# Two selective-scan instructions of 448 tokens joined into one of 898 columns, with the carried state in a column between them

## The chip, the cores and the metric

The kernel runs on one core of one Trainium2 chip. The metric is the device time of one execution in microseconds, from its first to its last instruction. The kernel before takes 8633.8 us, the median of three runs from 8621.33 to 8647.61. Engine names below: PE is the matrix engine, DVE the vector engine, ACT the scalar engine, POOL is GpSimd, and SP starts the transfers.

## The reference, cut to what matters

Four layers work on four images of 56 x 56 tokens and 96 channels. The last two are attention and a small feed-forward part. The first two hold a selective scan, and that scan fills nearly all of the time. Per image it runs in four directions (rows or columns, forward or backward), for 192 channels with 16 states each, over 3136 tokens:

```python
dt  = softplus(dts + dt_bias)
dA  = exp(dt * A)                 # one decay for each token, channel and state
dBu = dt * B * u                  # what a token adds
def step(h, inp):
    dA_l, dBu_l, C_l = inp
    h = dA_l * h + dBu_l          # the recurrence, token after token
    return h, einsum('bkdn,bkn->bkd', h, C_l)
_, ys = lax.scan(step, h0, (dA, dBu, Ct))
```

Everything around it (projections, convolutions, norms, the feed-forward parts) is matrix work and elementwise work, which the kernel runs in the gaps.

## The kernel before

The kernel cuts each direction into 7 steps of 448 tokens. A step has 8 rounds (two halves of the channels, four sets of states), which makes 2 layers x 4 images x 4 directions x 7 steps x 8 rounds = 1792 rounds. In a round 3 groups of 128 (channel, state) pairs are scanned, each in one DVE instruction over the tokens. One round consists of

- two or three products on DVE, `v = du * b` (L673). In 1204 rounds the third one is done ahead of time on POOL (L651);
- three scans on DVE, in place in `v`, with decays read from PSUM (L699);
- three exponentials on ACT, which write the next round's decays into PSUM as soon as the scan that read the old ones is through (L643);
- two small copies on ACT: the state that ends a step goes out to `carry` (L703), and the state that begins the next round's step comes in from `carry` (L658);
- the product with C on POOL over all three groups (L709), and on PE the sum over states.

```python
CS = 448
TOKENS = slice(1, CS + 1)
...
        da = [self.psum.tile([128, 512], F32, name=f"da{g}")[:, : CS + 2] for g in range(NG)]
        for t in da:
            nc.vector.memset(t, 0.0)

        def decay(n, g):
            ch, e, q = rounds[n]
            nc.scalar.activation(da[g][:, TOKENS], ch.dt[e][:, g], AF.Exp, scale=ch.par.na[:, e, q, g : g + 1])

        def begin(n):
            ch, e, q = rounds[n]
            b = self.spread_b(ch, q)
            v = sp.tile([128, NG, CS + 2], F32, name="v", bufs=3)
            ahead = NQ * e + q not in (OWN_TAIL if ch.l and ch.i else OWN)
            if ahead:
                nc.gpsimd.tensor_tensor(v[:, 2, TOKENS], ch.du[e][:, 2], ch.cb[q][:, 1], ALU.mult)
            return b, v, ahead

        def carried(n, v):
            ch, e, q = rounds[n]
            at = CS + 1 if ch.rev else 0
            if ch.step:
                nc.scalar.copy(v[:, :, at : at + 1], ch.par.carry[:, e, q].unsqueeze(2))
        ...
        for n, (ch, e, q) in enumerate(rounds):
            ...
            c = 1 if ch.step else 0
            way = slice(CS + c, 0, -1) if ch.rev else slice(1 - c, CS + 1)
            end = 1 if ch.rev else CS
            b, v, ahead = nxt
            for g in range(2 if ahead else 3):
                nc.vector.tensor_tensor(v[:, g, TOKENS], ch.du[e][:, g], b, ALU.mult)
            ...
            yield "F", n, r                    # other lanes may put ACT work here
            ...
            if more:
                nxt = begin(n + 1)
            ...
            for g in range(NG):
                if g == 1:
                    yield "C", n, r            # other lanes may put PE and DVE work here
                ...
                nc.vector.tensor_tensor_scan(
                    v[:, g, way], da[g][:, way], v[:, g, way], 0.0, ALU.mult, ALU.add
                )
                if g == 2 and ch.step < NCS - 1:
                    nc.scalar.copy(ch.par.carry[:, e, q].unsqueeze(2), v[:, :, end : end + 1])
                if more:
                    decay(n + 1, g)
                    if g == 0:
                        carried(n + 1, nxt[1])
            hc = sp.tile([128, NG, CS], F32, name="hc", bufs=3)
            nc.gpsimd.tensor_tensor(hc, v[:, :, TOKENS], ch.cb[q][:, 0].unsqueeze(1).to_broadcast([128, NG, CS]), ALU.mult)
```

The order of instructions on each engine is the order in which this code emits them. The waits between engines are set by the framework, from the overlap of the stretches of a tile that two instructions touch. "Lanes" are the other layers' parts (projections, norms, feed-forward), which are let in at the two `yield`s. A scan writes `h` over `v`. Where a step continues a direction, the column ahead of the first token holds the carried state, and since its decay is zero the scan starts from it.

Of the kernel before, what the change touches and what calls it, by code (L numbers as in the profile page):

```python
# [11 lines left out]
F32 = mybir.dt.float32  # L12
# [3 lines left out]
AF = mybir.ActivationFunctionType  # L16
ALU = mybir.AluOpType
# [9 lines left out]
NG = 3  # L27
NQ = 4
# [2 lines left out]
CR = CW // HS  # L31
NCW = L // CW
CS = 448
TOKENS = slice(1, CS + 1)
NCS = L // CS
RANK = (12, 6)
NW, LATE_NW = 13, 20
# [6 lines left out]
BANKS, LATE_BANKS = 2, 4  # L44
# [120 lines left out]
class Net:  # L165
# [25 lines left out]
    def late(self):  # L191

        self.scan_pool.close()
        self.wp = self.pool("late", bufs=2)
        self.nw, self.nwin, self.depth, self.banks = LATE_NW, LATE_DEPTH, LATE_DEPTH, LATE_BANKS
        tags = (("ps", BANKS), ("da0", 1), ("da1", 1), ("da2", 1), ("pp", 1), ("b", 1), ("y", 1))
        self.ring = cycle([t for t in tags for _ in range(t[1])])

    def ps(self):
# [395 lines left out]
    def scans(self):  # L595

        nc, sp = self.nc, self.sp
        chunks = []
        for l in range(2):
            for i in range(NB):
                for n, (orient, rev) in enumerate(ORDER[l]):
                    for step in range(NCS):
                        ch = Step()
                        ch.l, ch.i, ch.orient, ch.rev, ch.step = l, i, orient, rev, step  # L610
                        ch.k = 2 * orient + rev if l == 0 else orient + 2 * rev
                        ch.c = NCS - 1 - step if rev else step
                        ch.n, ch.first = n, n == 0 and step == 0
                        ch.skip = n == 0
                        ch.last = n == 3 and step == NCS - 1
                        for n_ in ("dt", "du", "cb", "dtc", "duc", "dtd", "dud"):
                            setattr(ch, n_, [])
                        chunks.append(ch)
        first, second = chunks[:2]
        self.parameters(first)  # L620
        self.inputs(first)
        self.project_step(first, 0)
        self.project_step(first, 1)
        for r in range(8):
            if r:
                self.prepare(Step(), first, r)
            self.prepare_on_scalar(first, r)
        self.parameters(second)
        self.project_step(second, 0)
        self.project_step(second, 1)  # L630
        rounds = [(ch, e, q) for ch in chunks for e in range(NE) for q in range(NQ)]
        nexts = dict(zip(chunks, chunks[1:]))
        afters = dict(zip(chunks, chunks[2:]))


        da = [self.psum.tile([128, 512], F32, name=f"da{g}")[:, : CS + 2] for g in range(NG)]
        for t in da:
            nc.vector.memset(t, 0.0)

        def decay(n, g):  # L640

            ch, e, q = rounds[n]
            nc.scalar.activation(da[g][:, TOKENS], ch.dt[e][:, g], AF.Exp, scale=ch.par.na[:, e, q, g : g + 1])  # L643

        def begin(n):
            ch, e, q = rounds[n]
            b = self.spread_b(ch, q)
            v = sp.tile([128, NG, CS + 2], F32, name="v", bufs=3)
            ahead = NQ * e + q not in (OWN_TAIL if ch.l and ch.i else OWN)
            if ahead:  # L650
                nc.gpsimd.tensor_tensor(v[:, 2, TOKENS], ch.du[e][:, 2], ch.cb[q][:, 1], ALU.mult)  # L651
            return b, v, ahead

        def carried(n, v):
            ch, e, q = rounds[n]
            at = CS + 1 if ch.rev else 0
            if ch.step:
                nc.scalar.copy(v[:, :, at : at + 1], ch.par.carry[:, e, q].unsqueeze(2))  # L658

        nxt = begin(0)  # L660
        self.exp_and_ln()
        self.tables = True
        for g in range(NG):
            decay(0, g)
        late = []
        for n, (ch, e, q) in enumerate(rounds):
            r = NQ * e + q
            c = 1 if ch.step else 0
            way = slice(CS + c, 0, -1) if ch.rev else slice(1 - c, CS + 1)
            end = 1 if ch.rev else CS  # L670
            b, v, ahead = nxt
            for g in range(2 if ahead else 3):
                nc.vector.tensor_tensor(v[:, g, TOKENS], ch.du[e][:, g], b, ALU.mult)  # L673
            self.prepare(ch, nexts.get(ch), r)
            self.half_round()
            far = afters.get(ch)
            strided = [1.5 + 1.5 * ch.orient] * (r % NQ == 2)
            if far and self.projected(far, r) in (0, 1):
                strided.append(1.5 + 1.5 * far.orient)
            self.spend((0.7, 0, 1.3, 1.3, 0, 0, 0, 0)[r], 1.3 * (r in (1, 3)) + sum(strided))  # L680
            yield "F", n, r
            self.prepare_on_scalar(nexts.get(ch), r)
            ended = late.pop(0) if len(late) == 2 else None
            if ended:
                self.keep_busy(ended[2])
            more = n + 1 < len(rounds)
            if more:
                nxt = begin(n + 1)
            if ended:
                self.add_up(*ended)  # L690
            self.prepare_ahead(afters.get(ch), r)
            self.half_round()
            for g in range(NG):
                if g == 1:
                    yield "C", n, r
                if g == 2 and ended and ended[2] == NQ - 1:
                    self.spend(0.6, 0)
                    self.keep_sums(*ended[:3])
                nc.vector.tensor_tensor_scan(  # L699
                    v[:, g, way], da[g][:, way], v[:, g, way], 0.0, ALU.mult, ALU.add  # L700
                )
                if g == 2 and ch.step < NCS - 1:
                    nc.scalar.copy(ch.par.carry[:, e, q].unsqueeze(2), v[:, :, end : end + 1])  # L703
                if more:
                    decay(n + 1, g)
                    if g == 0:
                        carried(n + 1, nxt[1])
            hc = sp.tile([128, NG, CS], F32, name="hc", bufs=3)
            nc.gpsimd.tensor_tensor(hc, v[:, :, TOKENS], ch.cb[q][:, 0].unsqueeze(1).to_broadcast([128, NG, CS]), ALU.mult)  # L709
            late.append((ch, e, q, hc))  # L710
        for ended in late:
            self.add_up(*ended)
        self.keep_sums(ch, e, q)
        yield "C", len(rounds), 0
# [624 lines left out]
```

## Time and profile before

| engine | busy us of 8626.1 | in the stage of the rounds, 120 to 8290 us |
|---|---|---|
| DVE | 7939.4 | 7846.7 of 8170 |
| POOL | 7594.3 | 7556.1 of 8170 |
| PE | 7475.5 | 7111.6 of 8170 |
| ACT | 5909.3 | 5686.5 of 8170 |

The first 120 us prepare the first image. The last 336 us are the end of the last lanes, after the last scan. Between them lie the 1792 rounds, 8164 us from the first round's scan to the last one's, or 4.56 us each. In a line of the profile's groups, the first number after the bar is the busy time in us, the next one the mean of one instruction in ns, and after the second bar stands the engine's idle time just before these instructions and who ended most of it.

### The profile page before, as it was taken

Reading aid. Unit: us, or ns where it says so; the run is one execution under the profiler, and the core shown is the slowest. Engines: PE = TensorE matmul, PEld = TensorE weight load, DVE = VectorE, ACT = ScalarE, POOL = GpSimd, SP = SyncE. Lnnn points to the kernel's source line nnn. Section 1 sums busy time; section 2 is a strip of 40 time slices with the busy share of each in tenths; the row PEclk is TensorE's granted clock in tenths of the full one; section 3 lists DMA queues with packets and bytes.
Section 4 is the critical chain, followed back from the end, with each engine's and each line's share of the span. In section 5 each row is a group of like instructions: output and inputs, shape, how many; then the busy total and the mean of one; then the engine's idle time right before and its main releaser. Section 6 shows DMA issues by size and latency. Waiting matters only on the chain. (4 is left out here: it accounts for less than half of the span.)

```text
span 8626.1 us, 120872 instructions
## 1 busy us (share of the span) xinstructions
PE 7475.5 (87%) x33459; PEld 2708.0 (31%) x33459; DVE 7939.4 (92%) x10933; ACT 5909.3 (69%) x12541; POOL 7594.3 (88%) x4075
## 2 busy tenths in 40 slices
PE   6788888898889888898889989988899888998997
PEld 3222223232333223232223223323233232333345
DVE  5999999999999999999999999999999999999951
ACT  5777667676777667776677756667766777667646
POOL 4888989999999999999999999999999999999940
PEclk8888889898999989998899989988899888998987
DMA  5677677677777777776777777667776677766731
GB/s 144 159 184 174 164 179 179 162 167 166 187 169 179 168 185 173 172 176 159 185 175 171 170 174 166 161 154 167 185 174 150 161 165 186 171 149 163 168 90 45
DMA packets 951340, 1417.89 MB, mean 164 GB/s; under 512 B 176578, under 2 KB 943812, under 8 KB 949796
## 3 DMA queue, kind: packets, MB, share of 16 engines
q1 hardware_dynamic: 949888, 1408.37, 68.6%
q8 instruction: 263, 4.31, 0.2%
q14 instruction: 417, 3.42, 0.2%
q10 hardware_dynamic: 772, 1.80, 0.1%
HBM read 1141.42 MB, written 268.14 MB: 163 GB/s over the span
## 5 line engine op out<-in xcount | busy, mean ns | idle before, releaser
L709 POOL TENSOR_TENSOR hc<-v,cb 128x1344 f32<-128x1344 f32 x1792 | 5168.2, 2885 | 499.4 <-DVE v L699 288.1
L699 DVE TENSOR_TENSOR_SCAN v<-da,v 128x449 f32<-128x449 f32 (+1 forms) x5376 | 5523.8, 1072 | 60.4 <-ACT v L658 33.2
L643 ACT ACTIVATE da<-dt,na 128x448 f32<-128x448 f32 x5376 | 3394.5, 633 | 1583.2 <-DVE v L699 1557.3
L673 DVE TENSOR_TENSOR v<-du,b 128x448 f32<-128x448 f32 x4172 | 2330.0, 605 | 136.5 <-PE b L580 50.0
L737 PE MATMUL y<-hc,four 128*32 128x448 f32 x14336 | 1959.6, 622 | 4.3 <-POOL hc L709 4.3
L580 PE MATMUL b<-cf,sel 128*128 128x448 bf16 x1792 | 682.6, 381 | 954.7 <-DVE v L673 949.9
L651 POOL TENSOR_TENSOR v<-du,cb 128x448 f32<-128x448 f32 x1204 | 1374.6, 1142 | 95.8 <-DMA cb<-cd 69.0
L724 PE MATMUL y<-w,zeros 128*96 128x448 bf16 x5117 | 1441.9, 399 | 0.0
L724 PEld LDWEIGHTS <-zeros 128*96 128x96 bf16 x5117 | 631.5, 134 | 1306.5 <-issue 1149.6
L737 PEld LDWEIGHTS y<-hc,four 128*32 128x32 f32 x14336 | 297.5, 114 | 1291.2 <-issue 917.7
L428 PE MATMUL pp<-U,wd 96*128 96x448 f32 x896 | 671.3, 836 | 9.1 <-DMA U<-u 9.1
L733 PE MATMUL y<-Y,ident 96*96 96x448 f32 x672 | 539.8, 892 | 42.3 <-ACT Y L744 23.6
L496 POOL TENSOR_TENSOR duc<-dtc,U 96x448 f32<-96x448 f32 x448 | 559.8, 1250 | 4.6 <-ACT dtc L490 4.6
L886 PE MATMUL ps<-win,dg 64*64 64x220 f32 (+9 forms) x1962 | 509.3, 454 | 0.0
L703 ACT COPY carry<-v 128x3 f32<-128x3 f32 x1536 | 299.2, 195 | 287.7 <-DVE v L699 286.9
L480 PE MATMUL pp<-cf,wd 12*96 12x448 f32 (+1 forms) x896 | 488.0, 627 | 1.1 <-ACT cf L467 1.0
L489 ACT ACTIVATE dtc<-pp,wd 96x448 f32<-96x448 f32 x448 | 279.3, 623 | 270.1 <-PE pp L480 267.7
L593 POOL TENSOR_TENSOR cf<-cf 64x448 f32<-64x448 f32 x448 | 417.5, 932 | 35.7 <-ACT cf L467 0.6
L744 ACT COPY Y<-y 96x448 f32<-96x448 f32 x448 | 339.3, 757 | 31.8 <-PE y L737 30.6
L886 PEld LDWEIGHTS ps<-win,dg 64*64 64x64 f32 (+2 forms) x1962 | 230.6, 158 | 329.9 <-issue 272.7
L580 PEld LDWEIGHTS <-sel 128*128 128x128 bf16 x1792 | 186.7, 104 | 350.2 <-issue 285.8
L733 PEld LDWEIGHTS y<-Y,ident 96*96 96x96 f32 x672 | 116.8, 184 | 553.2 <-ACT da L643 243.8
(426 smaller groups left out, 6066.0 us busy)
## 6 DMA issues: line engine op xcount, KB each, us to landing
cb<-cd SPq DMA_DIRECT2D x3584, 112.0 KB, 4.3
dt<-dd SPq DMA_DIRECT2D x1792, 168.0 KB, 4.4
du<-dd SPq DMA_DIRECT2D x1792, 168.0 KB, 4.2
dd<-dtc SPq DMA_DIRECT2D x448, 168.0 KB, 2.0
dd<-duc SPq DMA_DIRECT2D x448, 168.0 KB, 2.1
U<-u SPq DMA_DIRECT2D x112, 168.0 KB, 4.6
z<-w SPq DMA_DIRECT2D x56, 224.0 KB, 3.1
u<-w SPq DMA_DIRECT2D x56, 224.0 KB, 3.4
```

Of the source, the lines that this page charges most:

```text
L428: self.nc.tensor.matmul(ch.ps.rearrange("p (a b) -> p a b", b=HS), ch.par.wx[:, e], self.in_order(self.U[e], ch.orient, ch.c * CS, CS), st ...
L496: self.nc.gpsimd.tensor_tensor(du.rearrange("p (a b) -> p a b", b=HS), ch.dtc[e].rearrange("p (a b) -> p a b", b=HS), self.in_order(self.U ...
L580: self.nc.tensor.matmul(ps, self.sel[:, q], self.upper(ch.cf), start=True, stop=True)
L643: nc.scalar.activation(da[g][:, TOKENS], ch.dt[e][:, g], AF.Exp, scale=ch.par.na[:, e, q, g : g + 1])
L651: nc.gpsimd.tensor_tensor(v[:, 2, TOKENS], ch.du[e][:, 2], ch.cb[q][:, 1], ALU.mult)
L673: nc.vector.tensor_tensor(v[:, g, TOKENS], ch.du[e][:, g], b, ALU.mult)
L699: nc.vector.tensor_tensor_scan(v[:, g, way], da[g][:, way], v[:, g, way], 0.0, ALU.mult, ALU.add)
L709: nc.gpsimd.tensor_tensor(hc, v[:, :, TOKENS], ch.cb[q][:, 0].unsqueeze(1).to_broadcast([128, NG, CS]), ALU.mult)
L724: self.nc.tensor.matmul(self.y[:C], self.zeros, self.some, start=False, stop=False)
L733: nc.tensor.matmul(o, w, self.in_order(a, ch.orient, ch.c * CS, CS), start=True, stop=False)
L737: nc.tensor.matmul(self.y[32 * n : 32 * n + 32], self.four, hc[:, g], start=n == 3, stop=n == 3 or q == NQ - 1,)
L886: self.nc.tensor.matmul(o[:, a - r0 : e - r0, x0:x1], diag[:, tap], win[:, a + dy - lo : e + dy - lo, x0 + dx : x1 + dx], start=n == 0, st ...
```

## The change

The scans of groups 1 and 2 become one instruction. For that `v` loses its third dimension: it is a row of 3 x 449 + 1 columns, in which one column for the carried state and 448 tokens alternate. The decays of groups 1 and 2 lie in one tile over two adjacent PSUM banks, placed so that each exponential still writes within one bank. Between the two groups of decays stays one column with zero: there the running product is wiped out and the second group's carried state taken up. The column is now needed in every round, so where a direction begins the carried state is a copy of zeros (`none`), which the kernel before did without. The aim is to issue fewer instructions on the vector engine.

```diff
-TOKENS = slice(1, CS + 1)
+GW = CS + 1
...
-        tags = (("ps", BANKS), ("da0", 1), ("da1", 1), ("da2", 1), ("pp", 1), ("b", 1), ("y", 1))
+        tags = (("ps", BANKS), ("da0", 1), ("da", 1), ("pp", 1), ("b", 1), ("y", 1))
...
+        one = self.psum.tile([128, 512], F32, name="da0")[:, : GW + 1]
+        two = self.psum.tile([128, 1024], F32, name="da")[:, 511 - GW : 512 + GW]
+        factors = [one[:, 1:GW], two[:, 1:GW], two[:, 1 + GW : 2 * GW]]
+
+        def tokens(v):
+            return v[:, 1:].rearrange("p (g t) -> p g t", t=GW)[:, :, :CS]
...
-            v = sp.tile([128, NG, CS + 2], F32, name="v", bufs=3)
+            v = sp.tile([128, NG * GW + 1], F32, name="v", bufs=3)
...
         def carried(n, v):
             ch, e, q = rounds[n]
-            at = CS + 1 if ch.rev else 0
-            if ch.step:
-                nc.scalar.copy(v[:, :, at : at + 1], ch.par.carry[:, e, q].unsqueeze(2))
+            at = v[:, 1:] if ch.rev else v[:, : NG * GW]
+            at = at.rearrange("p (g t) -> p g t", t=GW)[:, :, CS if ch.rev else 0]
+            nc.scalar.copy(at.unsqueeze(2), ch.par.carry[:, e, q].unsqueeze(2) if ch.step else none)
...
-            for g in range(NG):
-                if g == 1:
+            for g, f, w in ((0, one, v[:, : GW + 1]), (1, two, v[:, GW:])):
+                if g:
                     yield "C", n, r
...
-                nc.vector.tensor_tensor_scan(
-                    v[:, g, way], da[g][:, way], v[:, g, way], 0.0, ALU.mult, ALU.add
-                )
-                if g == 2 and ch.step < NCS - 1:
-                    nc.scalar.copy(ch.par.carry[:, e, q].unsqueeze(2), v[:, :, end : end + 1])
+                way = slice(f.shape[1] - 1, 0, -1) if ch.rev else slice(0, f.shape[1] - 1)
+                nc.vector.tensor_tensor_scan(w[:, way], f[:, way], w[:, way], 0.0, ALU.mult, ALU.add)
+                if g and ch.step < NCS - 1:
+                    nc.scalar.copy(ch.par.carry[:, e, q].unsqueeze(2), tokens(v)[:, :, end : end + 1])
                 if more:
-                    decay(n + 1, g)
+                    for m in ((0,), (1, 2))[g]:
+                        decay(n + 1, m)
                     if g == 0:
                         carried(n + 1, nxt[1])
```

(The products and the product with C use `tokens(v)` in place of `v[:, :, TOKENS]`; these lines are cut.)

More of the change, by code (lines that the diff above doesn't have):

```diff
@@ L633, in scans @@
         afters = dict(zip(chunks, chunks[2:]))
-        da = [self.psum.tile([128, 512], F32, name=f"da{g}")[:, : CS + 2] for g in range(NG)]
-        for t in da:
-            nc.vector.memset(t, 0.0)
+        none = self.const.tile([128, NG, 1], F32, name="none")
+        nc.vector.memset(none, 0.0)
+        one = self.psum.tile([128, 512], F32, name="da0")[:, : GW + 1]
+        two = self.psum.tile([128, 1024], F32, name="da")[:, 511 - GW : 512 + GW]
+        nc.vector.memset(one, 0.0)
+        nc.vector.memset(two, 0.0)
+        factors = [one[:, 1:GW], two[:, 1:GW], two[:, 1 + GW : 2 * GW]]
+        def tokens(v):
+            return v[:, 1:].rearrange("p (g t) -> p g t", t=GW)[:, :, :CS]
         def decay(n, g):
             ch, e, q = rounds[n]
-            nc.scalar.activation(da[g][:, TOKENS], ch.dt[e][:, g], AF.Exp, scale=ch.par.na[:, e, q, g : g + 1])
+            nc.scalar.activation(factors[g], ch.dt[e][:, g], AF.Exp, scale=ch.par.na[:, e, q, g : g + 1])
         def begin(n):
@@ L647, in begin @@
             b = self.spread_b(ch, q)
-            v = sp.tile([128, NG, CS + 2], F32, name="v", bufs=3)
+            v = sp.tile([128, NG * GW + 1], F32, name="v", bufs=3)
             ahead = NQ * e + q not in (OWN_TAIL if ch.l and ch.i else OWN)
             if ahead:
-                nc.gpsimd.tensor_tensor(v[:, 2, TOKENS], ch.du[e][:, 2], ch.cb[q][:, 1], ALU.mult)
+                nc.gpsimd.tensor_tensor(tokens(v)[:, 2], ch.du[e][:, 2], ch.cb[q][:, 1], ALU.mult)
             return b, v, ahead
@@ L655, in carried @@
             ch, e, q = rounds[n]
-            at = CS + 1 if ch.rev else 0
-            if ch.step:
-                nc.scalar.copy(v[:, :, at : at + 1], ch.par.carry[:, e, q].unsqueeze(2))
+            at = v[:, 1:] if ch.rev else v[:, : NG * GW]
+            at = at.rearrange("p (g t) -> p g t", t=GW)[:, :, CS if ch.rev else 0]
+            nc.scalar.copy(at.unsqueeze(2), ch.par.carry[:, e, q].unsqueeze(2) if ch.step else none)
         nxt = begin(0)
+        carried(0, nxt[1])
         self.exp_and_ln()
@@ L667, in scans @@
             r = NQ * e + q
-            c = 1 if ch.step else 0
-            way = slice(CS + c, 0, -1) if ch.rev else slice(1 - c, CS + 1)
-            end = 1 if ch.rev else CS
+            end = 0 if ch.rev else CS - 1
             b, v, ahead = nxt
             for g in range(2 if ahead else 3):
-                nc.vector.tensor_tensor(v[:, g, TOKENS], ch.du[e][:, g], b, ALU.mult)
+                nc.vector.tensor_tensor(tokens(v)[:, g], ch.du[e][:, g], b, ALU.mult)
             self.prepare(ch, nexts.get(ch), r)
@@ L692, in scans @@
             self.half_round()
-            for g in range(NG):
-                if g == 1:
+            for g, f, w in ((0, one, v[:, : GW + 1]), (1, two, v[:, GW:])):
+                if g:
                     yield "C", n, r
[L696 to L699, printed above, removed]
-                    v[:, g, way], da[g][:, way], v[:, g, way], 0.0, ALU.mult, ALU.add
-                )
-                if g == 2 and ch.step < NCS - 1:
-                    nc.scalar.copy(ch.par.carry[:, e, q].unsqueeze(2), v[:, :, end : end + 1])
+                    if ended and ended[2] == NQ - 1:
+                        self.spend(0.6, 0)
+                        self.keep_sums(*ended[:3])
+                way = slice(f.shape[1] - 1, 0, -1) if ch.rev else slice(0, f.shape[1] - 1)
+                nc.vector.tensor_tensor_scan(w[:, way], f[:, way], w[:, way], 0.0, ALU.mult, ALU.add)
+                if g and ch.step < NCS - 1:
+                    nc.scalar.copy(ch.par.carry[:, e, q].unsqueeze(2), tokens(v)[:, :, end : end + 1])
                 if more:
-                    decay(n + 1, g)
+                    for m in ((0,), (1, 2))[g]:
+                        decay(n + 1, m)
                     if g == 0:
@@ L708, in scans @@
             hc = sp.tile([128, NG, CS], F32, name="hc", bufs=3)
-            nc.gpsimd.tensor_tensor(hc, v[:, :, TOKENS], ch.cb[q][:, 0].unsqueeze(1).to_broadcast([128, NG, CS]), ALU.mult)
+            nc.gpsimd.tensor_tensor(hc, tokens(v), ch.cb[q][:, 0].unsqueeze(1).to_broadcast([128, NG, CS]), ALU.mult)
             late.append((ch, e, q, hc))
```

## The prediction

> **What bounds the kernel now.** I read the busy shares first, then the stage of the rounds by itself, then the groups of instructions, and at last single rounds in the timeline. The page's slices and the stretches (the three rows are the start, the rounds and the end; columns PE, PEld, DVE, ACT, POOL) say where the time lies:
>
> ```profile
> DVE  5999999999999999999999999999999999999951
> POOL 4888989999999999999999999999999999999940
> ...
> 120.00:8290.00 8170.00, 7111.57 (x31932) 2486.02 (x31935) 7846.66 (x10624) 5686.54 (x12068) 7556.10 (x4031) 0.90 0.72 170
> ```
>
> In the rounds DVE is busy for 7846.7 of 8170 us (96%) and idle for 323 us; POOL is at 92.5%, ACT at 70%. So DVE sets the pace, with POOL close behind. The groups:
>
> ```profile
> L709 POOL TENSOR_TENSOR hc<-v,cb 128x1344 f32<-128x1344 f32 x1792 | 5168.2, 2885 | 499.4 <-DVE v L699 288.1
> L699 DVE TENSOR_TENSOR_SCAN v<-da,v 128x449 f32<-128x449 f32 (+1 forms) x5376 | 5523.8, 1072 | 60.4 <-ACT v L658 33.2
> L643 ACT ACTIVATE da<-dt,na 128x448 f32<-128x448 f32 x5376 | 3394.5, 633 | 1583.2 <-DVE v L699 1557.3
> L673 DVE TENSOR_TENSOR v<-du,b 128x448 f32<-128x448 f32 x4172 | 2330.0, 605 | 136.5 <-PE b L580 50.0
> L651 POOL TENSOR_TENSOR v<-du,cb 128x448 f32<-128x448 f32 x1204 | 1374.6, 1142 | 95.8 <-DMA cb<-cd 69.0
> ```
>
> The scan hardly waits (60.4 us over 5376), the exponentials wait for the scans. Now one backward round, first its DVE, then ACT, then POOL:
>
> ```profile
> 2553.17 3.05 DVE L699 TENSOR_TENSOR_SCAN v<-da,v 128x449 f32<-128x449 f32 x3
> 2556.14 1.12 DVE L673 TENSOR_TENSOR v<-du,b 128x448 f32<-128x448 f32 x2
> 2557.19 3.05 DVE L699 TENSOR_TENSOR_SCAN v<-da,v 128x449 f32<-128x449 f32 x3
> ...
> 2554.29 0.64 ACT L643 ACTIVATE da<-dt,na 128x448 f32<-128x448 f32 x1 [1.85 <-DVE v L699]
> 2554.87 0.18 ACT L658 COPY v<-carry 128x3 f32<-128x3 f32 x1
> ...
> 2556.18 1.13 POOL L651 TENSOR_TENSOR v<-du,cb 128x448 f32<-128x448 f32 x1
> ```
>
> Three scans take 2556.14 - 2553.17 = 2.97 us from issue to issue, 0.99 each; the 1.07 us of the group view overlap. Two products take 1.05 us. A round with two products is 4.02 us (2557.19 - 2553.17), and the third product's 0.52 makes it 4.54. The carried state (L658) is in at 2555.05, over a microsecond before the round's products begin, and it is needed only by the scan. And one forward round whose ACT also has lane work:
>
> ```profile
> 1806.70 1.66 DVE L673 TENSOR_TENSOR v<-du,b 128x448 f32<-128x448 f32 x3
> 1808.27 1.08 DVE L699 TENSOR_TENSOR_SCAN v<-da,v 128x449 f32<-128x449 f32 x1
> ...
> 1803.55 1.28 ACT L1033 ACT_TABLE_LOAD   x1
> 1804.85 0.63 ACT L1033 ACTIVATE w<-ps,c 128x448 f32<-128x448 f32 x1
> 1805.50 1.28 ACT L768 ACT_TABLE_LOAD   x1
> 1806.80 0.64 ACT L643 ACTIVATE da<-dt,na 128x448 f32<-128x448 f32 x1
> 1807.37 0.18 ACT L658 COPY v<-carry 128x3 f32<-128x3 f32 x1
> ```
>
> Lane work with two table loads holds ACT from 1803.55 to 1806.78. The first group's exponential and the carried copy come after it, at 1807.55, while DVE has been in its products since 1806.70. Today that is harmless: the scan begins at 1808.27.
>
> [...]
>
> **The change part by part.**
>
> 1. *One scan less per round.* 898 columns are 2 x 449, [...] **-98 us**, all on DVE, the bound. In the steps that begin a direction the scans grow from 448 to 449 columns, 2 ns each, and 256 copies of zeros of 0.18 us are added on ACT: nothing that counts.
>
> 2. *Both exponentials after the joined scan.* Before, the second group's ran beside the third scan; now ACT begins it one scan later and ends both some 0.64 us (one exponential) later. They are needed when the joined scan starts, one scan (0.99 us) earlier than the third group's were. Put on the recorded starts round by round, the joined scan would come too early in 288 rounds, by 119 us in sum. Most of these rounds also have a stall of point 3 ahead of it, so I count half: **+60 us**. The later ACT lane work counts in point 4.
>
> 3. *New waits around the carried copy.* In the built program of the change the copy's target is a strided view of a flat row, and it is ordered against everything between its first and last column. In forward rounds the columns are 0, 449 and 898, so the **first product** of the round now waits for the copy on ACT. In backward rounds they are 449, 898 and 1347, so the **second product** waits for the copy, and the copy waits for POOL's third product where there is one (it writes columns 899 to 1346). None of these waits is in the program before, where the scan alone waited for the copy. Again round by round on the recorded starts, with 0.18 us for the copy[...]:
>  - 895 forward rounds: the copy would be late in 215, by 185 us in sum. In the forward round shown, 1807.55 against 1806.70 makes 0.9 us.
>  - 294 backward rounds without POOL's product: 47 late, 34 us.
>  - 602 backward rounds with it: 335 late, 338 us. In the one shown POOL ends at 2557.31, the copy could end at 2557.54, and the second product began at 2556.65: 0.9 us. POOL's lateness carries over from round to round, and a stall that has pushed DVE back once is not paid again in the next round, so I choose half: 169 us.
>  In sum **+388 us**.
>
> 4. *What shifts behind that.* In the 215 late forward rounds the exponentials of point 2 push lane work, and so the next copy, up to 0.64 us later: at most 138 us, I take half, **+69 us**. In backward rounds ACT stands still for POOL, 1.7 us on average over the 602 rounds, mostly in time in which it waits for scans today. In return, part of the present 323 us of idle DVE is swallowed by the new stalls; I take a third, **-100 us**.
>
> 5. *The end.* The lanes after the last scan rotate over seven PSUM tiles in place of eight. 336 us; I count nothing.
>
> Sum: -98 + 60 + 388 + 69 - 100 = +319, from 8633.8 to 8953. Because two of the halves are chosen and repeated rounds recover more easily than single ones, I round down to **8930 us**.
>
> **Rivals.**
>
> - *The waits are met in time and the saving comes through.* For it: ACT is idle for 30% of the rounds, and the median forward copy would be 1 us early. Then 8634 - 98 = 8536, under 2% in any case. Against it: a quarter of forward and over half of POOL-fed backward rounds are late in the recorded order, and DVE has no slack to hide that.
> - *POOL takes over as the bound.* The loop over two rounds, product with C 2.89, product ahead 1.14, copy 0.18, second product 0.53, first scan 0.99, [...] is 7.95 us, or 3.97 per round; each POOL side job (0.93 or 1.25 us) adds to it, up to 4.6. That is as long as today's 4.56. If it closes in every backward round, the full 338 us count and more: 9100 to 9150.
> - *Only the decays matter*, the new copy waits being covered by them: then about 8634 - 98 + 119 = 8655, within 2%.
> - *Crossing the bank costs something in the scan.* Nothing in the trace tells; 0.1 us per round would be 180 us, on top.
>
> **Range and chances.** With the whole of the absorbed halves gone the sum is about +150 (8790); with all of point 3 and 4 counted it is near +500 (9130). So 8780 to 9120. Slower by over 2% means above 8806: 0.88. Within 2%: 0.10. Faster by over 2%[...]: 0.02.
>
> **What would show it.** In the profile of the changed kernel: [...] DVE's products idle for 300 to 600 us with ACT's carried copy as the releaser (136.5 us in all now, 50.0 of it by PE's b); ACT's copy waiting for POOL's third product by hundreds of us; DVE's share down to some 88 to 89%; rounds near 4.7 us. Were the products' wait for ACT under 100 us, point 3 would be wrong; a joined scan of 2.1 us or more would bear out the bank; an idle joined scan waiting for exponentials by over 200 us would mean that point 2 is the larger one.

## The result and the profile after

The changed kernel takes 8963.65 us (median of 4 runs, 8960.8 to 8966.01) against 8640.7 before (the 8633.8 that the prediction starts from was the median of three of these four runs): a ratio of 1.0377, with a 95% interval of 1.0358 to 1.0396. It is slower by 3.8%, inside the predicted range and 34 us above the predicted time.

The same rows of the page as before, DVE and POOL over 40 slices, and then the start, the rounds and the end (only the middle stretch is shown):

```profile
DVE  5898999989999999989998899999999999999951
POOL 4788888888888888888888898888988888888840
...
120.00:8620.00 8500.00, 7260.69 (x31923) 2529.53 (x31922) 7804.14 (x8831) 5797.40 (x12323) 7283.03 (x4031) 0.88 0.63 163
```

DVE has lost its solid row of nines, and POOL has gone from nines to eights. In the rounds DVE works for 7804 of 8500 us, where it was 7847 of 8170: 43 us less work and 373 us more idleness. The groups of the kernel after:

```profile
L716 POOL TENSOR_TENSOR hc<-v,cb 128x1344 f32<-128x1344 f32 x1792 | 4883.9, 2726 | 1099.0 <-DVE v L707 760.1
L707 DVE TENSOR_TENSOR_SCAN v<-da,v 128x449 f32<-128x449 f32 (+1 forms) x3584 | 5450.0, 1546 | 53.6 <-ACT da L651 33.1
L680 DVE TENSOR_TENSOR v<-du,b 128x448 f32<-128x448 f32 x4172 | 2359.9, 608 | 546.2 <-ACT v L666 464.8
L666 ACT COPY v<-carry 128x3 f32<-128x3 f32 x1536 | 283.6, 185 | 578.5 <-POOL v L659 576.4
```

and two of the kernel before, whose releasers count below:

```profile
L699 DVE TENSOR_TENSOR_SCAN v<-da,v 128x449 f32<-128x449 f32 (+1 forms) x5376 | 5523.8, 1072 | 60.4 <-ACT v L658 33.2 <-POOL v L651 24.7 <-ACT da L643 1.0
L658 ACT COPY v<-carry 128x3 f32<-128x3 f32 x1536 | 277.1, 180 | 3.0 <-POOL hc L709 1.9
```

The idle time before the products (L680) has gone from 136.5 to 546.2 us, and 464.8 of it ends with ACT's copy of the carried state (L666). That copy in turn has waited 576.4 us for POOL's third product (L659). In the kernel before the copy waited 3.0 us in all, and ACT is not named among those for whom the products waited. The scans themselves wait as little as they did, 53.6 us for 60.4, but for others: no longer for the copy (33.2 us before), and 33.1 us for exponentials, where it was 1.0. Kept apart by shape, the scans are

```profile
L707 DVE TENSOR_TENSOR_SCAN v<-da,v 128x898 f32<-128x898 f32 x1792 | 3597.5, 2008 | 53.6 <-ACT da L651 33.1 <-POOL v L659 12.2 <-POOL hc L716 2.8
L707 DVE TENSOR_TENSOR_SCAN v<-da,v 128x449 f32<-128x449 f32 x1792 | 1942.7, 1084 | 0.0
```

so the scan over two PSUM banks takes 2008 ns, 936 more than the 1072 of one scan before. The next instruction usually starts 1919 ns after it does, where two scans before take 983 each in this way, 1966 in all: it costs no more than two scans. A backward round, DVE, then ACT, then POOL:

```profile
3181.19 0.60 DVE L680 TENSOR_TENSOR v<-du,b 128x448 f32<-128x448 f32 x1
3182.66 0.62 DVE L680 TENSOR_TENSOR v<-du,b 128x448 f32<-128x448 f32 x1 [0.87 <-ACT v L666]
3183.20 1.08 DVE L707 TENSOR_TENSOR_SCAN v<-da,v 128x449 f32<-128x449 f32 x1
...
3179.39 0.64 ACT L651 ACTIVATE da<-dt,na 128x448 f32<-128x448 f32 x1 [0.55 <-DVE v L707]
3182.44 0.20 ACT L666 COPY v<-carry 128x3 f32<-128x3 f32 x1 [2.40 <-POOL v L659]
...
3180.26 0.93 POOL L593 TENSOR_TENSOR cf<-cf 64x448 f32<-64x448 f32 x1
3181.27 1.13 POOL L659 TENSOR_TENSOR v<-du,cb 128x448 f32<-128x448 f32 x1
```

POOL, held up by a side job (L593), ends its product at 3182.40. ACT has stood still for 2.40 us behind it, then copies three columns, and at 3182.66 DVE may begin the second product, 0.87 us late. A forward round, where the product waits for a copy that stands behind lane work with two table loads:

```profile
1346.56 1.15 DVE L680 TENSOR_TENSOR v<-du,b 128x448 f32<-128x448 f32 x2 [1.52 <-ACT v L666]
...
1342.00 1.28 ACT L1012 ACT_TABLE_LOAD   x1
1343.30 1.16 ACT L1012 ACTIVATE w<-ps,b 128x448 f32<-128x448 f32 x2
1344.48 1.28 ACT L775 ACT_TABLE_LOAD   x1
1345.77 0.64 ACT L651 ACTIVATE da<-dt,na 128x448 f32<-128x448 f32 x1
1346.35 0.18 ACT L666 COPY v<-carry 128x3 f32<-128x3 f32 x1
```

To compare kernels I use one more reading of the same trace. A scan or a product on DVE is recorded some 90 ns beyond the moment at which the next starts (before: a scan with 1072 ns, the next start after 983; a product with 605, the next start after 512), so short waits show no gap at all. I therefore took the distances from start to start. For every kind of neighbours (product after product, scan after product and so on) the shortest usual distance (the third percentile) counts as work, and what lies beyond it as a wait of the later instruction. In us, over the stage from the first scan to the last:

| kernel | work | products wait | scans wait | lanes wait | stage |
|---|---|---|---|---|---|
| before | 7561 | 152 | 238 | 215 | 8166 |
| after | 7485 | 606 | 218 | 189 | 8498 |

All instructions of the lanes count as one kind here, so some 150 us of the scans' column and 85 of the lanes' are really longer lane instructions. They are in both rows and drop out of the differences.

The join saves 76 us of work. The products' waits grow by 454 us. Scans and lanes wait 46 us less. -76 + 454 - 46 = +332, the difference of the stages.

### The profile page after: what moved, and what is told of

It reads as the page before. It is cut to its first block, busy times and chain, and to the rows that moved or that the text cites. A ratio compares the mean times of both kernels' runs of the same rounds, so it can differ in the third digit from the quotient of the medians.

```text
span 8963.2 us, 116531 instructions
## 1 busy us (share of the span) xinstructions
PE 7633.7 (85%) x33459; PEld 2756.2 (31%) x33459; DVE 7896.8 (88%) x9141; ACT 6022.9 (67%) x12798; POOL 7323.3 (82%) x4075
## 5 line engine op out<-in xcount | busy, mean ns | idle before, releaser
L716 POOL TENSOR_TENSOR hc<-v,cb 128x1344 f32<-128x1344 f32 x1792 | 4883.9, 2726 | 1099.0 <-DVE v L707 760.1
L707 DVE TENSOR_TENSOR_SCAN v<-da,v 128x449 f32<-128x449 f32 (+1 forms) x3584 | 5450.0, 1546 | 53.6 <-ACT da L651 33.1
L680 DVE TENSOR_TENSOR v<-du,b 128x448 f32<-128x448 f32 x4172 | 2359.9, 608 | 546.2 <-ACT v L666 464.8
L744 PE MATMUL y<-hc,four 128*32 128x448 f32 x14336 | 2008.6, 637 | 1.7 <-POOL hc L716 1.6
L731 PE MATMUL y<-w,zeros 128*96 128x448 bf16 x5117 | 1472.9, 406 | 0.0
L659 POOL TENSOR_TENSOR v<-du,cb 128x448 f32<-128x448 f32 x1204 | 1369.0, 1137 | 84.3 <-DMA cb<-cd 52.5
L666 ACT COPY v<-carry 128x3 f32<-128x3 f32 x1536 | 283.6, 185 | 578.5 <-POOL v L659 576.4
L593 POOL TENSOR_TENSOR cf<-cf 64x448 f32<-64x448 f32 x448 | 417.7, 932 | 35.3 <-ACT cf L467 0.3
```

The lines of the kernel that those rows point to most:

```text
L659: nc.gpsimd.tensor_tensor(tokens(v)[:, 2], ch.du[e][:, 2], ch.cb[q][:, 1], ALU.mult)
L680: nc.vector.tensor_tensor(tokens(v)[:, g], ch.du[e][:, g], b, ALU.mult)
L707: nc.vector.tensor_tensor_scan(w[:, way], f[:, way], w[:, way], 0.0, ALU.mult, ALU.add)
L716: nc.gpsimd.tensor_tensor(hc, tokens(v), ch.cb[q][:, 0].unsqueeze(1).to_broadcast([128, NG, CS]), ALU.mult)
L731: self.nc.tensor.matmul(self.y[:C], self.zeros, self.some, start=False, stop=False)
L744: nc.tensor.matmul(self.y[32 * n : 32 * n + 32], self.four, hc[:, g], start=n == 3, stop=n == 3 or q == NQ - 1,)
```

## The experiments

Theory A, that of the prediction: the loss comes from the waits around the carried copy, which come with the flat row and not with the join. Rival B: from both exponentials standing after the joined scan and being needed for the next one. Rival C: from the longer scan over two banks. Each kernel's ratio is to the kernel before, run on the same chip beside it.

**e1: the join without the new waits.** `v` is a three-dimensional tile again (rows of 450 columns), in three fixed buffers, and the joined scan goes over two rows of it. With the rows of before, POOL's product with C is back at 2883 ns from 2726; e7 below shows what that is worth.

```diff
-            v = sp.tile([128, NG * GW + 1], F32, name="v", bufs=3)
+            v = vs[n % 3]            # three tiles [128, NG, CS + 2], zeroed once
...
-            at = v[:, 1:] if ch.rev else v[:, : NG * GW]
-            at = at.rearrange("p (g t) -> p g t", t=GW)[:, :, CS if ch.rev else 0]
-            nc.scalar.copy(at.unsqueeze(2), ch.par.carry[:, e, q].unsqueeze(2) if ch.step else none)
+            at = GW - 1 if ch.rev else 0
+            nc.scalar.copy(v[:, :, at : at + 1], ch.par.carry[:, e, q].unsqueeze(2) if ch.step else none)
...
-            for g, f, w in ((0, one, v[:, : GW + 1]), (1, two, v[:, GW:])):
+            for g, f, w in ((0, one, v[:, 0]), (1, two, v.rearrange("p g t -> p (g t)")[:, GW:])):
```

> The joined scan and the late exponentials stay; v is kept in three dimensions again (rows of 450 columns, in three fixed buffers), so that neither the products wait for the carried copy nor the copy for POOL's third product. Theory A (the new waits around the carried copy are the loss): the loss goes and the fixed cost stays saved, 8640 - 98 + 60 for the late exponentials = about 8600 us (8560 to 8660), the products' idle time back to 140 us or less. Rival B (the late exponentials are the loss): 8850 us or more, with the joined scan idle for them by over 200 us. Rival C (a scan across two banks costs more than two scans): 8800 us or more with the joined scan above 2.1 us.

Measured: 8778.25 us, ratio 1.0172 (1.0157 to 1.0188). Its groups by shape:

```profile
L709 DVE TENSOR_TENSOR_SCAN v<-da,v 128x899 f32<-128x899 f32 x1792 | 3604.2, 2011 | 148.9 <-ACT da L654 102.1 <-POOL v L662 36.6 <-POOL hc L718 7.9
L682 DVE TENSOR_TENSOR v<-du,b 128x448 f32<-128x448 f32 x4172 | 2330.9, 605 | 127.7 <-PE b L580 32.9 <-POOL duc L496 30.9 <-DMA du<-dd 30.1
L709 DVE TENSOR_TENSOR_SCAN v<-da,v 128x449 f32<-128x449 f32 x1792 | 1942.7, 1084 | 106.7 <-ACT v L668 106.5
```

The products no longer wait for ACT, and 185 us of the loss are gone (8964 to 8778). But the expected 8600 is missed: the kernel is still 1.7% behind, because now the scans wait, the first for the copy (106.5 us) and the joined one for exponentials (102.1 us). In the change those two waits lay mostly hidden behind the products' wait (33.1 us of the second shows there). So the new waits are a loss, and there is a second one under them.

**e2: the new waits without the join.** The kernel before, its three scans and its exponentials in their places, with only the flat row and the copy's strided view of it (and the zeros where a direction begins).

```diff
-            v = sp.tile([128, NG, CS + 2], F32, name="v", bufs=3)
+            v = sp.tile([128, NG * GW + 1], F32, name="v", bufs=3)
...
-            at = CS + 1 if ch.rev else 0
-            if ch.step:
-                nc.scalar.copy(v[:, :, at : at + 1], ch.par.carry[:, e, q].unsqueeze(2))
+            at = v[:, 1:] if ch.rev else v[:, : NG * GW]
+            at = at.rearrange("p (g t) -> p g t", t=GW)[:, :, CS if ch.rev else 0]
+            nc.scalar.copy(at.unsqueeze(2), ch.par.carry[:, e, q].unsqueeze(2) if ch.step else none)
```

> Three scans and the exponentials as before; only v is a flat row and the carried copy is the strided view of it, so that its waits are those of the change. Theory A: slower than before by what the change lost and without what the join saved, about 8990 us (8900 to 9080), with the products idle for some 450 us because of the copy. Rivals B and C: the time of before, 8620 to 8680 us.

Measured: 8926.97 us, ratio 1.0343 (1.0327 to 1.0358).

```profile
L707 DVE TENSOR_TENSOR_SCAN v<-da,v 128x449 f32<-128x449 f32 x5376 | 5522.1, 1073 | 5.5 <-POOL v L658 4.2
L680 DVE TENSOR_TENSOR v<-du,b 128x448 f32<-128x448 f32 x4172 | 2358.9, 607 | 475.8 <-ACT v L665 347.8 <-issue 47.8 <-DMA du<-dd 25.6
```

Nothing is joined here, and nearly the whole loss is there: 3.4 of 3.8%. The scans hardly wait (5.5 us); the products do, for the copy. Rivals B and C would have left the time as it was. By direction, mean rounds grow from 4585 to 4670 ns forward and from 4532 to 4767 ns backward, over 896 rounds each 76 and 210 us.

**e8: more of the same waits.** The change, with three-dimensional `v`, where the copy writes the first and the last column of each group's row in one instruction. Now every round's first product waits for the copy, and the copy for POOL's product wherever there is one; in the change it was half of each.

```diff
-            nc.scalar.copy(at.unsqueeze(2), ch.par.carry[:, e, q].unsqueeze(2) if ch.step else none)
+            start = ch.par.carry[:, e, q].unsqueeze(2) if ch.step else none
+            nc.scalar.copy(v[:, :, :: GW - 1], start.to_broadcast([128, NG, 2]))
```

> The change with more of the same waits: the carried copy writes both end columns of each group's row, so that in every round the first product waits for the copy, and the copy waits for POOL's third product in every round that has one (in the change half of each). Theory A: slower still, 9080 to 9350 us, with the products idle for the copy by 600 us or more. If the waits around the copy are not what costs: about 8960 us or, like e1, 8780 us.

Measured: 9323.53 us, ratio 1.0788 (1.0764 to 1.0811). Its two longest waits of this kind:

```profile
ACT v L665 <- POOL v L659: 1354.5, 914, 14.1
...
DVE v L679 <- ACT v L665: 824.1, 760, 5.1
```

In the change they are 682.4 us (the 576.4 above and 106 for the copies of zeros) and 464.8. They have grown to 2.0 and 1.8 times, and the loss to 2.1 times, 7.9% for 3.8%. With e1 and e2 this settles that the waits around the copy are the larger part.

**e3 and e5: the two halves of rival B, one by one.** e3 is the kernel before with the second group's exponential after the third scan. e5 is the kernel before with the third group's scan second, so that POOL's product is needed one scan earlier, while each exponential still follows its own scan.

```diff
 # e3
-                    decay(n + 1, g)
+                    for m in ((0,), (), (1, 2))[g]:
+                        decay(n + 1, m)
 # e5
-            for g in range(NG):
+            for at, g in enumerate((0, 2, 1)):
```

> The kernel before, with one edit: the exponential of the second group comes after the third scan, as it does in the change. Theory A: about 60 us more, 8700 us (8650 to 8770). Rival B: 8850 us or more.

Measured: 8717.66 us, ratio 1.0109 (1.0092 to 1.0126).

> The kernel before with its three scans in the order first, third, second group: POOL's product is needed one scan (0.99 us) earlier, as in the change; every exponential still follows its own scan. Theory G (the earlier need of POOL's product counts): in the recorded trace 62 rounds were short by 74 us, so 8670 to 8720 us with scans waiting for POOL by 50 to 100 us. Rival (only the exponentials count): 8620 to 8660 us.

Measured: 8646.91 us, ratio 1.0013 (1.0005 to 1.0022).

Late exponentials alone cost 1.1%, near what theory A allowed and far from what rival B needed. The earlier need of POOL's product costs next to nothing, though it was late on paper in 62 rounds by 74 us. Theory G of e5 fell: the scans wait for POOL 40.2 us in place of 24.7.

```profile
L699 DVE TENSOR_TENSOR_SCAN v<-da,v 128x449 f32<-128x449 f32 (+1 forms) x5376 | 5525.9, 1073 | 74.9 <-POOL v L651 40.2 <-ACT v L658 32.4 <-ACT da L643 1.0
```

**e10: late and needed early.** e5 and e3 at once: scans in the order first, third, second group, both exponentials after the last, second group's first. The second scan in order then needs the exponential that comes last, as the joined scan does, with nothing joined and no new wait.

> Three scans, no new waits, nothing joined: the order of the scans is first, third, second group, and both late exponentials stand after the last scan, second group's first. So the second scan in order needs the exponential that comes last, as the joined scan does. Theory H (what e1 loses is that both exponentials come after the last scan and both are needed for the next one): e1 without the saving of the join, 8778 + 75 = about 8850 us (8800 to 8890), with the second scan held back by some 120 us more than before. Rival F (a longer scan is harmful in itself): the time of e3, 8700 to 8740 us.

Measured: 8793.89 us, ratio 1.0188 (1.0169 to 1.0207), against 1.0172 for e1.

```profile
L699 DVE TENSOR_TENSOR_SCAN v<-da,v 128x449 f32<-128x449 f32 x4608 | 4754.2, 1075 | 187.8 <-ACT v L658 85.0 <-ACT da L643 73.8 <-POOL v L651 22.8
```

The two waits of e1, for the copy and for exponentials, are here as well. So what e1 loses is there without any join: rival F, a long scan harmful in itself, fell, as did C. But the expected 8850 is missed as well. Read as in the table, in us:

| kernel | work | products wait | scans wait | lanes wait | stage |
|---|---|---|---|---|---|
| e1 | 7486 | 155 | 442 | 223 | 8306 |
| e2 | 7568 | 522 | 173 | 189 | 8453 |
| e10 | 7559 | 121 | 417 | 233 | 8330 |

The join saves e1 73 us of work against e10, but the stage is only 24 us shorter; scans, products and lanes of e1 wait 49 us more than those of e10. Between these two, work taken from DVE comes back as waits. Nor do the losses add up: e2 alone loses 3.4% and e10 alone 1.9%, but the change, which has both and a saving of 1%, loses 3.8%. One kind of stall covers part of the other.

**e4, e11 and e12: the join at the front.** If the joined scan stands first and the third scan alone at the end, two exponentials and the copy run beside that third scan. e12 differs from e4 in two points (copy ahead of the exponentials, tokens at an even column), and e11 from e12 in one (POOL makes the first group's product, DVE the second's and third's).

```diff
 # e4, against e1
-            for g, f, w in ((0, one, v[:, 0]), (1, two, v.rearrange("p g t -> p (g t)")[:, GW:])):
+            for g, f, w in ((0, two, v.rearrange("p g t -> p (g t)")[:, : 2 * GW]), (1, one, v[:, 2])):
...
-                    for m in ((0,), (1, 2))[g]:
+                    for m in ((0, 1), (2,))[g]:
                         decay(n + 1, m)
                     if g == 0:
                         carried(n + 1, nxt[1])
 # e12: carried(n + 1, nxt[1]) ahead of the decays
 # e11, also
-                nc.gpsimd.tensor_tensor(v[:, 2, 2 : 2 + CS], ch.du[e][:, 2], ch.cb[q][:, 1], ALU.mult)
+                nc.gpsimd.tensor_tensor(v[:, 0, 2 : 2 + CS], ch.du[e][:, 0], ch.cb[q][:, 1], ALU.mult)
...
-            for g in range(2 if ahead else 3):
+            for g in range(1 if ahead else 0, NG):
```

> As e1 (no new waits), but the joined scan is that of the first and second group and stands first; the third group's scan stands alone at the end, so that two of the three exponentials and the carried copy run beside it, and POOL's product is needed as late as in the kernel before. Theory D (what is left of the loss in e1, 145 us in place of a gain of 98, comes from exponentials and POOL's product being needed a scan earlier and ready a scan later): most of it goes, 8540 to 8640 us, scans idle for under 120 us. Rival F (a longer scan on DVE is itself harmful, whatever stands around it): 8750 us or more.

Measured: 8804.73 us, ratio 1.0184 (1.0164 to 1.0204).

```profile
L709 DVE TENSOR_TENSOR_SCAN v<-da,v 128x899 f32<-128x899 f32 x1792 | 3632.5, 2027 | 275.0 <-ACT v L668 160.2 <-ACT da L654 1.4 <-ACT na L464 0.5
```

Theory D fell: e4 is no better than e1. The joined scan waits 160 us for the copy, which this edit had put behind two exponentials; most of the 113 us that are left in the line have the cause found with e12.

> e4 with the carried copy ahead of the two exponentials and tokens at an even column; POOL makes the third product as before. Against e11 it tells what POOL's product costs against the wait for DVE's own product. If the copy was the larger part of e4's loss (164 us of idle scan): 8640 to 8700 us with the wait for the copy under 30 us; if the wait for DVE's own last product and for the exponentials is: 8730 to 8790 us.

Measured: 8758.26 us, ratio 1.0139 (1.0124 to 1.0154).

> e4 mended in three places: the carried copy goes ahead of the two exponentials, tokens begin at an even column, and POOL makes the first group's product in place of the third's, so that a product of another group stands between the last product that the joined scan needs and the scan. In e4 the joined scan was held back by 381 us. If the copy and the wait for DVE's own product cause that, 8570 to 8660 us; the danger is POOL's product, needed two scans earlier (late in 317 rounds by 239 us in the recorded trace before): then 8700 to 8800 us with scans waiting for POOL by 150 us or more.

Measured: 8662.02 us, ratio 1.0024 (1.0016 to 1.0031). The joined scans of e12 and then of e11:

```profile
L709 DVE TENSOR_TENSOR_SCAN v<-da,v 128x903 f32<-128x903 f32 x1792 | 3647.7, 2036 | 248.0 <-ACT da L654 134.7 <-DVE v L682 0.9 <-ACT v L668 0.9
```

```profile
L709 DVE TENSOR_TENSOR_SCAN v<-da,v 128x903 f32<-128x903 f32 x1792 | 3639.6, 2031 | 211.4 <-ACT da L654 162.3 <-POOL v L662 41.7 <-ACT rs L811 1.8
```

Copy first: its wait is gone (160.2 to 0.9 us), but the exponentials, now behind it, take most of its place (134.7), and e12 gains little. The last step, from e12 to e11, gains 1.1%. In e12 the joined scan follows at once on the product that it reads. From that product's start to the scan's it usually takes 718 ns in the 1204 rounds with two products, and 531 ns in those with three, where the last product belongs to another group. In e11 it is 531 ns in both. 1204 x 187 ns = 225 us of e12 went into this, and e11 trades it for POOL's 42 us. Not all of that comes through: the first scan's wait, read as in the table, falls only from 354 to 239 us and the stage by 113, as the waits for exponentials and for POOL's product grow. A join done in this way comes out level with the kernel before, 0.2% behind; of its waits, that for the exponentials (162 us) is the largest. But e11 also has two helps that need no join, the even columns and lane work let in after two groups; e13 below has both with three scans.

**e6, e7 and e13: POOL's columns, and a version that beats both.** In the change POOL's product with C fell from 2885 to 2726 ns. e6 is the kernel before with tokens from column 2 of a row of 452, in place of column 1 of 450; e7 is e1 with the same; e13 is e6 with the lanes let in after the second scan.

```diff
 # e6
-TOKENS = slice(1, CS + 1)
+TOKENS = slice(2, CS + 2)
...
-            v = sp.tile([128, NG, CS + 2], F32, name="v", bufs=3)
+            v = sp.tile([128, NG, CS + 4], F32, name="v", bufs=3)
 # e13, also
-                if g == 1:
+                if g == 2:
                     yield "C", n, r
```

> The kernel before, with every group's tokens at an even column of v (row of 452, tokens from column 2; nothing else). In the change POOL's product with C takes 2726 ns in place of 2885, and one of its three groups begins at an even column (1, 450, 899; before 1, 451, 901). Theory E (POOL reads a group faster from an even column): three times the gain, 2885 - 3 x 159 = 2408 ns, POOL busy some 850 us less, and because DVE is the bound the time only 0 to 100 us lower, 8540 to 8640 us. Rival (the row's pitch of 449 or the lower load on DVE makes the difference): 2885 ns and 8640 us as before.

Measured: 8611.45 us, ratio 0.9971 (0.9964 to 0.9979).

```profile
L709 POOL TENSOR_TENSOR hc<-v,cb 128x1344 f32<-128x1344 f32 x1792 | 4595.7, 2565 | 1025.3 <-DVE v L699 624.3 <-ACT Y L744 71.7 <-PE y L737 67.7
```

Not the 2408 ns of theory E, but 2565: 573 us less work on POOL (5168.2 before), and 0.3% of time, since DVE is the bound.

> e1 with every group's tokens at an even column (rows of 452), so that POOL's product with C takes about 2565 ns as in e6, in place of 2883. If POOL's lateness is a good part of what e1 loses, 8680 to 8730 us; if it is the order on ACT, 8745 to 8775 us (the gain of e6, some 20 us, or less).

Measured: 8767.05 us, ratio 1.0143 (1.0126 to 1.0160). Its scans are a few columns longer, which adds 25 us of work by the table's reading (7511 against e1's 7486); the waits fall by 33 us. POOL's lateness is thus a small part of what e1 loses. That the rest is the order on ACT is what e10 supports.

> Three scans as in the kernel before, tokens at an even column as in e6, and the lanes' DVE work let in after the second scan instead of after the first, where it stood in e11 and e12: there it was held back by 120 us in place of 215, because ACT's part of it had one scan more to finish. If that is what helps: e6 less some 70 to 95 us, 8540 us (8510 to 8590). If the wait only moves to the third scan: 8600 to 8630 us as e6.

Measured: 8574.43 us, ratio 0.9927 (0.9909 to 0.9944). The lanes' part of DVE waits 149 us in place of e6's 210, as I take it because what ACT has to do for it has one scan longer; that is a little less than hoped for. The wait isn't merely moved to a scan: the scans wait 211 us in all, 225 in e6, though the products wait 175 us for 149. It is the fastest of all, below the kernel before by 0.7%, and has nothing joined. Set against it, e11 is 1.0% behind (ratios 1.0024 and 0.9927): by this comparison even the best of these joins costs more than it saves, and e11 owes its level time to the two helps. The two kernels differ in the order on ACT and in POOL's group as well, so the 1.0% is not the long scan alone.

## Why the prediction was right

The time was right (8930 for 8964), and so was the mechanism; the terms of the sum were off in both directions.

1. *One scan less.* Predicted -98, measured -76 us of work. The -98 was my estimate; no run before the change had shown what a join saves. The usual distances from a scan's start to the next start were 1002, 983 and again 983 ns before, and are 1002 and 1919 ns after, so 47 ns a round. A column more takes 2 ns (before, 981 ns from start to start with 448 columns and 983 with 449). At 2008 ns the scan over two banks stays under the 2.1 us that were to bear out a cost of the bank.
2. *Late exponentials.* Predicted +60 in the sum. In the change the scans idle 33.1 us for exponentials, 1.0 before. The scans' waits as a whole fell by 20 us, because the first scan's wait for the copy now stands with the products. By itself the step is worth more than I had it: 1.1% late (e3), 1.9% late and needed early (e10). I took half on the ground that the stalls of point 3 cover it; they cover more than half.
3. *Waits around the copy.* Predicted +388, measured +454 as waits of the products in the change and +370 in e2. By direction the products' waits grew by 211 us forward and 243 backward in the change (185 and 203 predicted), and by 129 and 241 in e2. In e2, which has the new waits alone, the forward sum was too large and the backward one, with its half, too small; with the late exponentials both were too small. The hand-overs, from the end of POOL's product to the start of the copy that waits for it and from the copy's end to DVE's product, usually take 32 ns each (after).
4. *What shifts, and what is swallowed.* Predicted +69 and -100 beside the +60 of point 2, together +29. Measured: lanes -26 and scans -20, together -46. In e2, without point 2, scans and lanes wait 65 and 26 us less, so the -100 for what is swallowed was about right. What the late exponentials push to later stands in part in the forward waits of point 3, 211 us in the change for 129 in e2; it can't be told apart further.
5. *The end.* The time from the last scan's start to the end went from 340.8 to 346.5 us, 6 us for a count of nothing.

The sums are +319 predicted and +332 measured. That they are so close is partly luck: point 3 was too small by 66, points 2 and 4 together too large by 75, and point 1 took credit for 22 us that it didn't have. Of the rivals, the saving that comes through is refuted by the time and by e2, POOL as the bound by its share (down to 85.7% in the rounds: 7283 of 8500 us), the bank by the scan's 2008 ns. In the loop of 7.95 us that spoke for POOL, the instructions come to 7.65 us with the joined scan at its measured 1919 ns; the rest was an estimate for the hand-overs. "Only the decays matter" named a loss of the right kind but the wrong place: it appears when the new waits are gone, in e1.

The signs that I named hold: products idle for 546 us, mostly by the copy; the copy waiting for POOL for 576 us; DVE at 88%; rounds of 4.74 us. The scans' busy time fell by 74 us.

Theory A's figure for e1, a time near 8600, was wrong by 180 us. It followed from the +60 of point 2, sized for a kernel in which another stall stands ahead. That the joined kernel without new waits would still lose was not foreseen.

## What to carry to other kernels

When a tile is laid out anew, look in the built program at who now waits for whom: here the strided view of a flat row was ordered against everything between its ends, and its three columns cost 3.4% (e2), nearly four times the 76 us of work that the join saved. Joining two scans on the bound engine saved 47 ns a round here, while it moved everything that hung on the first part to the end of the whole, and everything that fed the second part to its start; count both before counting the saving. Stalls overlap: taking one away may only uncover the next, so each needs its own experiment, alone and on top.

## What the runs showed of the hardware that I had not expected

- POOL's product of 128 x 1344 takes 2885 ns with the three groups at columns 1, 451 and 901, 2726 at columns 1, 450 and 899 (2724 in e2, with three scans), and 2565 at columns 2, 454 and 906. The steps are 159 and 161 ns. One third of the groups at an even column gave the first step and all three only the second, so an even column isn't the whole rule, and what is stays open. POOL's product that writes `v` did not change (1142, 1137 and 1137 ns).
- A scan that reads what the product just ahead of it on the same engine has written usually started 718 ns after that product's start (e12); with another group's product in between, it started 531 ns after the one in between (e12, e11). Of the 187 ns only some 103 are a gap between the records, since the recorded product lasts 0.61 us; in e12 they make 111 us of the joined scan's 248.0 us of idle time, with no releaser named.
